# Statistics by channel tiles, the last q/k products behind v's third tile, the second mean's steps together: one change to a three-stage image kernel

## The chip, the cores and the metric

The kernel runs on one core of a Trainium2 chip. The metric is the device time of one execution in microseconds; a kernel's time is the median over several executions.

## What is computed

The input x has 384 channels of 192 x 192 pixels, in float32. Two layers follow each other, each with a residual sum, and each preceded by a group normalization without scale (32 groups of 12 channels).

```
def gn(v): ...                                   # 32 groups: (v - mean) / sqrt(var + 1e-5)

# layer 0, on gn(x)
qkv = einsum('bchw,oc->bohw', x, w_qkv) + b_qkv          # 1x1 convolution, 384 -> 1152
qkv = max over 2x2 pixels                                 # 96 x 96
qkv = depthwise 3x3 convolution(qkv) + b_dw
q, k, v = split(qkv)                                      # 8 heads of 48 channels, over 9216 pixels
attn = (q / |q|) @ (k / |k|)^T * temperature              # 48 x 48 per head
out = sum over i of a_i * topk_softmax(attn, k_i) @ v     # k_i = 24, 32, 36, 38
out = gelu(out), each pixel repeated 2x2
x = x + einsum(out, w_proj) + b_proj

# layer 1, on gn(x)
xb = sign(gn(x)), each channel moved by -3 to 3 pixels along the row
x = x + einsum(xb, sign(weight)) + bias
```

## The kernel before

**Units.** x is cut into 24 units of 8 rows (`UR`), 1536 pixels (`UPX`); a unit holds three channel tiles of 128 partitions (`CT`), 2304 KB in all. The order of the stages on the core is: statistics of x, one pass over all units for q and k, one pass for v (with the softmax in its first units and the attention products in the others), and a last stage that projects, takes signs, multiplies for layer 1 and stores.

**Statistics (L219 to L294).** Units are loaded from 23 down to 0, each as one transfer except the first and the last, which are loaded in three parts, one for each channel tile. Every third unit goes wholly to ScalarE (ACT), which runs Identity and Square over each tile with a running sum (L239); the others go wholly to VectorE (DVE) in nine `bn_stats` of 512 pixels (L248), and after every fourth such unit each tile is aggregated (L250). Sums of both kinds are put together in six DVE steps (L263 to L269), a product with the group indicator adds the channels of a group (`group_sums`, L198), a short chain makes mean and reciprocal deviation per group (L274 to L280, with `inv_sqrt`), and `spread` (L203) brings both back to channels. DVE scales the weights wq by the deviation (L287), the first tile first. The mean's share of the bias comes from nine tiny products of `wg` with `shift` (`bqps`, L293), and DVE adds it to bq (L294). The pools of this part are then closed, and their memory is used by the next one.

**The q/k pass (L353 to L436).** `qkv_unit` (L313) makes one channel tile m of one unit: three blocks of pixels, three accumulated products each (L321) into one of three PSUM buffers, a maximum over 2 x 2 pixels on DVE (L328) that evicts a block, the bias on ACT (L335), and the depthwise convolution of nine steps, the first on ACT (L342), eight on DVE (L344). The result is transposed in 32 x 32 blocks on DVE (L383), and 16 DMAs on the SP queue bring the blocks of q or k to where TensorE (PE) can read them (`moved`, L401). `products(u)` (L412) is the product of q and k over a unit's pixels, 12 matmuls accumulated in three PSUM banks `gram`; in the loop it is issued one unit late, and that of the last unit is left to `gathered()`.

**The v pass (L571 to L641).** The same `qkv_unit` with tiles m = 0 to 2 for v. In unit 0, after m = 1, `gathered()` (L440 on) issues the last products and copies `gram` to `gsb`, and `group_sums` of the projection's bias gives `bg1` (L630, L631). From unit 1 on `softmaxes` (L449 on) is advanced by one step after each tile; its first steps sum the squares `ssq` (L455) into memory that belonged to the q/k pass, take the reciprocal root, and make `rk` (L465 to L468).

**What sets the order.** Up to here the framework's scheduler orders the instructions of each engine by its own estimate of the time; what the program issues later may be put earlier. The end of the v pass (L642 to L660) and the last stage (L771 on) are marked `manual_schedule`: there each engine runs in the order of the program. `order` of the units in the last stage starts with the two of `FIRST`, whose projection is made at L648 to L657 in the qkv buffers.

**The second mean (L650 to L660).** After the last attention product PE does the projection of m = 0, then m = 1, then the group product of the attention's sums (`wg1` with `om`, L655), then m = 2, then `spread`; DVE makes `om` (L651), `gm` (L656), `nmean1` (L660), and adds each projected tile to x in two steps (L568). The signs (L723, on ACT) wait for `nmean1`.

**The last stage.** For each unit: `summed` projects three tiles (`yps`, L559) and adds them (L568); `signed` makes the signs on ACT, and GpSimd (POOL) moves some channels (L701 to L715); `finished` makes the layer-1 products (L743) and adds them (L751); `stored` (L757) stores a finished unit from the ACT queue, and refills its memory from the SP queue with a unit that is still to come. The first units are stored and refilled tile by tile. The last two units are stored tile by tile from the SP queue as each tile is done (L755).

Of the kernel before, what the change touches and what calls it, by code (L numbers as in the profile page):

```python
# [10 lines left out]
F32 = mybir.dt.float32  # L11
# [9 lines left out]
P = 128  # L21
C = 384
# [125 lines left out]
def conv_preact_kernel(ctx: ExitStack, tc: tile.TileContext, a: dict, out: bass.AP):  # L148
# [65 lines left out]
    osum = ap.tile([P, CT, NAB], F32, name="osum")  # L214
    aT = right("aT").tile([P, CT, C], F32, name="aT")
    wq = right("wq").tile([P, CT, 3 * C], F32, name="wq")


    kept = {}  # L219
    with tc.tile_pool(name="p1", bufs=1, side="right") as p1, tc.tile_pool(name="p1ps", bufs=2, space=PSUM) as psp:  # L220
        stats = [p1.tile([P, CT, BATCH * (UPX // 512) * 6], F32, name=f"stats{i}") for i in range(NB)]
        mv = p1.tile([P, CT, NB, 2], F32, name="mv")
        acc = p1.tile([P, CT, 2, NU // SHARE], F32, name="acc")
        wg = p1.tile([NG, 3 * C], F32, name="wg")
        seen = 0
        for i in range(NU):
            u = NU - 1 - i
            xt = unit(u, parts=CT if u in (0, NU - 1) else 1)
            if u < KEEP:
                kept[u] = xt  # L230
            if i == 0:
                nc.scalar.dma_start(small, a["small"])
                nc.scalar.dma_start(indT, a["indT"])
                nc.scalar.dma_start(wq, a["w_qkvT"].rearrange("(t p) o -> p t o", p=P))
            if i % SHARE == 0:
                for t in range(CT):
                    for k, f in enumerate((AF.Identity, AF.Square)):
                        junk = p1.tile([P, UPX], BF16, name="junk")
                        nc.scalar.activation(  # L239
                            junk, xt[:, t], f, accum_out=acc[:, t, k, i // SHARE : i // SHARE + 1]  # L240
                        )
            else:
                b, k = divmod(seen, BATCH)
                seen += 1
                for t in range(CT):
                    for j in range(UPX // 512):
                        at = (k * (UPX // 512) + j) * 6
                        nc.vector.bn_stats(stats[b][:, t, at : at + 6], xt[:, t, j * 512 : (j + 1) * 512])  # L248
                    if k == BATCH - 1:
                        nc.vector.bn_aggr(mv[:, t, b, :], stats[b][:, t, :])  # L250
# [11 lines left out]
        more = p1.tile([P, CT, 2], F32, name="more")  # L262
# [12 lines left out]
        gv = p1.tile([NG, 2], F32, name="gv")  # L275
        nc.vector.tensor_scalar_mul(gv[:, 0:1], gs[:, 0:1], -1.0)
        var = p1.tile([NG, 1], F32, name="var")
        nc.vector.scalar_tensor_tensor(var, gs[:, 0:1], gv[:, 0:1], gs[:, 1:2], ALU.mult, ALU.add)
        nc.vector.tensor_scalar_add(var, var, 1e-5)
        inv_sqrt(p1, gv[:, 1:2], var, 1, "s0", NG)  # L280
        ps = psp.tile([P, CT, 2], F32, name="spread")
        spread(ps, gv)
        nc.vector.tensor_copy(rstd0, ps[:, :, 1])

        for c0, c1 in ((0, P), (P, 2 * C), (2 * C, 3 * C)):
            for t in range(CT):
                nc.vector.tensor_scalar_mul(wq[:, t, c0:c1], wq[:, t, c0:c1], rstd0[:, t : t + 1])  # L287
        nc.vector.tensor_copy(nmean0, ps[:, :, 0])
        shift = p1.tile([NG, 1], F32, name="shift")
        nc.vector.tensor_mul(shift, gv[:, 0:1], gv[:, 1:2])  # L290
        ps = psp.tile([P, NM], F32, name="bqps")
        for m in range(NM):
            nc.tensor.matmul(ps[:, m : m + 1], wg[:, m * P : (m + 1) * P], shift, start=True, stop=True)  # L293
        nc.vector.tensor_add(bq, bq, ps)  # L294
# [17 lines left out]

    def qkv_unit(pqkv, xt, u, m, pl, parts):  # L313

# [3 lines left out]
        for r0, nr, c0, ncol in BLOCKS:  # L318
            ps = pqkv.tile([P, 512], F32, name="qkv")
            for t in range(CT):  # L320
# [32 lines left out]
    with tc.tile_pool(name="p2w", bufs=1, side="right") as wp, tc.tile_pool(  # L353
# [52 lines left out]
        def products(u):  # L406

            n, nk, q, k = of_unit(u)
            for i in range(nk):
                L = min(P, n * WP - i * P)  # L410
                for t in range(CT):
                    nc.tensor.matmul(  # L412
                        gram[t][:, : BN[t] * B],
# [157 lines left out]
    with ExitStack() as vs:  # L571
# [34 lines left out]
        for u in range(NU):  # L606
# [10 lines left out]
            for m in range(CT):  # L617
# [24 lines left out]
        with tc.manual_schedule():  # L642
# [13 lines left out]
            nc.vector.tensor_scalar(gm, ps, -1.0 / (GRP * NPX), bg1, ALU.mult, ALU.add)  # L656
# [3 lines left out]
            nc.vector.tensor_add(nmean1, nmean0, ps[:, :, 0])  # L660

    att.close()


    with end:
# [68 lines left out]
        def finished(i):  # L734
# [3 lines left out]
            for m in range(CT):  # L738
                for r0 in range(0, UR, 4):
# [118 lines left out]
```

## Time and profile before

| | before |
|---|---|
| median of 4 runs | 2288.18 us (2286.95 to 2289.35) |
| profiled execution | 2288.53 us |
| its span, first to last instruction | 2286.7 us |
| granted TensorE clock, mean | 0.966 |
| PE busy | 2099.9 us (92%), 6135 instructions |
| DVE busy | 1903.4 us (83%), 3269 |
| ACT busy | 819.3 us (36%), 1418 |
| POOL busy | 211.4 us (9%), 338 |
| DMA | 300.30 MB, 208727 packets, mean 131 GB/s |

The profile is of one execution. Times are in microseconds from the start of the span. In the timeline a row gives start, duration, engine, line and operation; "out<-in" are tiles of the program, "x13" says how many instructions of a kind were run together in the row, and in brackets stand the idle time of the engine before the row and what ended it. PE is TensorE's products, PEld its weight loads, and the ending q (SPq, ACTq) means a queue that issues DMAs. One matmul in float32 shows as two records on PE. "Granted clock" is the share of full speed that TensorE was given. The stages lie at 0 to 161 (statistics), 161 to 1346 (q and k), 1346 to 1968 (v) and from there to the end (last stage). One execution of an unchanged kernel differs from another by about 2 us, as the four runs show.

### The profile page before, as it was taken

Reading aid. Unit: us, or ns where it says so; the run is one execution under the profiler, and the core shown is the slowest. Engines: PE = TensorE matmul, PEld = TensorE weight load, DVE = VectorE, ACT = ScalarE, POOL = GpSimd, SP = SyncE. Lnnn points to the kernel's source line nnn. Section 1 sums busy time; section 2 is a strip of 40 time slices with the busy share of each in tenths; the row PEclk is TensorE's granted clock in tenths of the full one; section 3 lists DMA queues with packets and bytes.
Section 4 is the critical chain, followed back from the end, with each engine's and each line's share of the span. In section 5 each row is a group of like instructions: output and inputs, shape, how many; then the busy total and the mean of one; then the engine's idle time right before and its main releaser. Section 6 shows DMA issues by size and latency. Waiting matters only on the chain.

```text
span 2286.7 us, 19474 instructions
## 1 busy us (share of the span) xinstructions
PE 2099.9 (92%) x6135; PEld 993.2 (43%) x6135; DVE 1903.4 (83%) x3269; ACT 819.3 (36%) x1418; POOL 211.4 (9%) x338
## 2 busy tenths in 40 slices
PE   1029999999999999999999979999999999989998
PEld 0014444444444444444444434444444444445554
DVE  4667888888888888888888878986788887879998
ACT  5532222222222222222222212225323333487775
POOL 0000000000000000000000000000000000276674
PEclk7559999999999999999999989999999999999999
DMA  9962222222222232222222222004222212289996
GB/s 397 418 261 61 65 64 70 72 95 71 65 64 70 72 95 70 65 64 71 74 93 71 64 48 86 38 31 177 83 83 80 86 42 85 81 335 404 420 411 248
DMA packets 208727, 300.30 MB, mean 131 GB/s; under 512 B 162000, under 2 KB 164848, under 8 KB 208624
## 3 DMA queue, kind: packets, MB, share of 16 engines
q1 hardware_dynamic: 197936, 243.46, 30.6%
q10 hardware_dynamic: 10688, 55.61, 6.0%
q8 instruction: 48, 0.79, 0.1%
q14 instruction: 55, 0.45, 0.1%
HBM read 213.68 MB, written 56.62 MB: 118 GB/s over the span
## 4 chain that ended last, share of the span: by engine, by line
PE 77%; DVE 11%; DMA 8%; ACT 2%; issue 1%; SPq 1%; ACTq 0%; POOL 0%; POOLq 0%; DVEq 0%
PE qkv L321 65%; DMA xt<-in_x_dram 7%; PE l1ps L743 5%; DVE chunk L344 4%; PE yps L559 3%; PE gram L412 3%; DVE pooled L328 2%; PE ops L594 2%; DVE xt L568 2%; DVE dw L344 1%; DVE stats L248 1%; DMA out_dram<-xt 1%; ACT signs L723 1%; DVE xt L751 0%; SPq L401 0%
## 5 line engine op out<-in xcount | busy, mean ns | idle before, releaser
L321 PE MATMUL qkv<-xt,wq 128*128 128x512 f32 x3888 | 1681.9, 593 | 0.3 <-DVE small L294 0.3
L321 PEld LDWEIGHTS qkv<-xt,wq 128*128 128x128 f32 x3888 | 736.4, 190 | 920.2 <-issue 823.9
L344 DVE SCALAR_TENSOR_TENSOR dw<-pooled,small,dw 128x384 f32<-128x384 f32 (+2 forms) x1152 | 709.1, 616 | 118.8 <-ACT dw L342 93.7
L328 DVE TENSOR_REDUCE pooled<-qkv 128x128 f32<-128x512 f32 x648 | 442.9, 685 | 71.5 <-PE qkv L321 71.0
L344 DVE SCALAR_TENSOR_TENSOR chunk<-pooled,small,chunk 128x384 f32<-128x384 f32 (+3 forms) x696 | 370.5, 546 | 74.7 <-ACT chunk L342 57.3
L346 ACT COPY pooled<-pooled 128x196 f32<-128x196 f32 x207 | 73.6, 356 | 764.5 <-DVE dw L344 543.0
L335 ACT ACTIVATE pooled<-pooled,small 128x384 f32<-128x384 f32 x216 | 133.0, 616 | 407.6 <-DVE pooled L328 400.1
L723 ACT ACTIVATE signs<-xt,nmean 64x1536 fp8e4<-64x1536 f32 x144 | 226.5, 1573 | 63.2 <-PE yps L559 51.6
L743 PE MATMUL l1ps<-signs,wb 128*128 128x384 fp8e4 x864 | 150.5, 328 | 6.6 <-POOL signs L715 4.5
L568 DVE SCALAR_TENSOR_TENSOR xt<-yps,small,xt 128x768 f32<-128x768 f32 x132 | 127.9, 1013 | 25.6 <-PE yps L559 19.2
L559 PE MATMUL yps<-chunk,wpr 128*128 128x384 f32 x396 | 136.5, 490 | 6.9 <-DVE xt L568 6.9
L751 DVE SCALAR_TENSOR_TENSOR xt<-l1ps,small,xt 128x768 f32<-128x768 f32 x144 | 135.6, 1009 | 6.1 <-ACT signs L723 4.0
L248 DVE BATCH_NORM_STATS2 stats<-xt 128x6 f32<-128x512 f32 x144 | 87.2, 676 | 60.6 <-DMA xt<-in_x_dram 60.6
L198 PE MATMUL gsps<-sums,small 128*32 128x2 f32 x6 | 0.5, 196 | 128.2 <-DVE sums L269 128.2
L433 ACT ACTIVATE sq<-dw 128x384 bf16<-128x384 f32 (+2 forms) x144 | 75.3, 523 | 117.0 <-DVE dw L344 117.0
L743 PEld LDWEIGHTS <-wb 128*128 128x128 fp8e4 x864 | 84.1, 97 | 74.3 <-issue 16.4
L302 POOL MEMSET pooled<- 128x196 f32 x9 | 2.4, 265 | 1171.9 <-DVE dw L344 1154.4
L342 ACT ACTIVATE dw<-pooled,small 128x384 f32<-128x384 f32 (+2 forms) x144 | 100.5, 698 | 2.3
L559 PEld LDWEIGHTS yps<-chunk,wpr 128*128 128x128 f32 x396 | 72.6, 190 | 62.4 <-PE yps L559 15.6
L239 ACT ACTIVATE junk<-xt 128x1536 bf16<-128x1536 f32 x48 | 71.1, 1482 | 52.1 <-DMA xt<-in_x_dram 50.9
L383 DVE STREAM_TRANSPOSE blocks<-dw 128x384 f32<-128x384 f32 (+1 forms) x144 | 82.0, 569 | 3.4
L412 PE MATMUL gram<-room 128*128 128x160 f32 (+3 forms) x438 | 68.1, 309 | 15.4 <-DMA room<-blocks 15.4
(117 smaller groups left out, 640.4 us busy)
## 6 DMA issues: line engine op xcount, KB each, us to landing
xt<-in_x_dram SPq DMA_DIRECT2D x83, 2304.0 KB, 13.2
out_dram<-xt ACTq DMA_DIRECT2D x19, 2304.0 KB, 13.9
room<-blocks SPq DMA_DIRECT2D x736, 36.0 KB, 2.0
xt<-in_x_dram SPq DMA_DIRECT2D x18, 768.0 KB, 8.5
out_dram<-xt ACTq DMA_DIRECT2D x9, 768.0 KB, 7.9
out_dram<-xt SPq DMA_DIRECT2D x6, 768.0 KB, 6.6
wq<-in_w_qkvT_dram ACTq DMA_DIRECT2D x1, 1728.0 KB, 15.2
room<-blocks SPq DMA_DIRECT2D x32, 48.0 KB, 2.1
```

The lines of the kernel that those rows point to most:

```text
L248: nc.vector.bn_stats(stats[b][:, t, at : at + 6], xt[:, t, j * 512 : (j + 1) * 512])
L321: nc.tensor.matmul(ps, wq[:, t, m * P : (m + 1) * P], x4[:, t, r0 : r0 + nr, c0 : c0 + ncol], start=(t == 0), stop=(t == CT - 1),)
L328: nc.vector.tensor_reduce(pl[:, 2 + r0 // 2 : 2 + (r0 + nr) // 2, 1 + c0 // 2 : 1 + (c0 + ncol) // 2], ps.rearrange("p (i a j b) -> p i j ...
L335: nc.scalar.activation(new, new, AF.Identity, bias=bq[:, m : m + 1])
L342: nc.scalar.activation(acc2, src, AF.Identity, bias=bdw[:, m : m + 1], scale=wdw[:, m, 0:1])
L344: nc.vector.scalar_tensor_tensor(acc2, src, wdw[:, m, k : k + 1], acc2, ALU.mult, ALU.add)
L412: nc.tensor.matmul(gram[t][:, : BN[t] * B], q[:L, t, i], k[:L, B0[t] : B0[t] + BN[t], i], start=u == 0 and i == 0, stop=u == NU - 1 and i ...
L559: nc.tensor.matmul(ps, wpr[:, t, m * P : (m + 1) * P], o[:, t, :], start=(t == 0), stop=(t == CT - 1),)
L568: nc.vector.scalar_tensor_tensor(x5[:, m, r], yb, bpr[:, m : m + 1], x5[:, m, r], ALU.add, ALU.add)
L723: nc.scalar.activation(rows_of(sg, p, SAT[t] - HSHIFT[t][h]), xt[p, t, :].rearrange("p (r w) -> p r w", w=W), AF.Sign, bias=nmean1[p, t : ...
L743: nc.tensor.matmul(ps[:, j, : 2 * W], wb[:, t, m * P : (m + 1) * P], rows_of(sg, slice(0, P), SAT[t])[:, r0 + 2 * j : r0 + 2 * j + 2], sta ...
L751: nc.vector.scalar_tensor_tensor(blk, ps[:, :, : 2 * W], bl1[:, m : m + 1], blk, ALU.add, ALU.add)
```

## The change

Five things are edited:

- **Statistics by channel tiles.** In every unit, ACT takes tile t = u mod 3 and DVE the other two, instead of whole units to one of them. ACT's sums are scaled as they are made, and all sums go into one array `part`, which has a further column with 0 and the 1e-5; three DVE steps are left for the reduction. Unit 1, too, is loaded in three parts. `wg` is put into memory of the later `aT`, and `shift` into the pool `att`, so that both outlive this part.
- **The bias** becomes a function, called after the third block of the first tile of unit 0; its products go into a buffer of the qkv ring.
- **The last products** of q and k: `gathered()` is called after m = 2, not m = 1, and these products are kept in program order. In the order of instructions of the changed kernel, PE has all 27 matmuls of v's unit 0 and then the 12 products; before, it had one of the products ahead of m = 1 and eleven behind it. The products for `bg1` stand at the very start of the kernel.
- **The second mean**: after m = 0, `wg1` with `om` and `spread` follow each other; m = 1 and m = 2 come behind them, on PE and on DVE.
- **The last store**: the last tile of the last unit is stored in two halves of 384 KB, each after its own sum.

```
-            xt = unit(u, parts=CT if u in (0, NU - 1) else 1)
+            xt = unit(u, parts=CT if u in (0, 1, NU - 1) else 1)
...
-            if i % SHARE == 0:
-                for t in range(CT):
-                    for k, f in enumerate((AF.Identity, AF.Square)):
...
-                        nc.scalar.activation(
-                            junk, xt[:, t], f, accum_out=acc[:, t, k, i // SHARE : i // SHARE + 1]
-                        )
-            else:
-                b, k = divmod(seen, BATCH)
...
+            for t in range(CT):
+                if t == u % SHARE:
+                    at = NB + i // SHARE
+                    for k, f, scale in ((0, AF.Identity, measure), (1, AF.Square, measure**0.5)):
+                        junk = p1.tile([P, UPX], BF16, name="junk")
+                        nc.scalar.activation(junk, xt[:, t], f, scale=scale, accum_out=part[:, t, k, at : at + 1])
+                    continue
+                b, k = divmod(seen[t], BATCH)
+                seen[t] += 1
...
+                if k == BATCH - 1:
+                    nc.vector.bn_aggr(part[:, t, :, b], stats[b][:, t, :])
...
-        nc.vector.tensor_reduce(more, acc, AX.X, ALU.add)
-        nc.vector.tensor_mul(sq, mv[:, :, :, 0], mv[:, :, :, 0])
-        nc.vector.tensor_add(sq, sq, mv[:, :, :, 1])
-        nc.vector.tensor_reduce(sums[:, :, 0], mv[:, :, :, 0], AX.X, ALU.add)
-        nc.vector.tensor_reduce(sums[:, :, 1], sq, AX.X, ALU.add)
-        nc.vector.scalar_tensor_tensor(sums, more, 1.0 / (BATCH * UPX), sums, ALU.mult, ALU.add)
+        nc.vector.tensor_mul(sq, part[:, :, 0, :NB], part[:, :, 0, :NB])
+        nc.vector.tensor_add(part[:, :, 1, :NB], part[:, :, 1, :NB], sq)
+        nc.vector.tensor_reduce(sums, part, AX.X, ALU.add)
...
-        nc.vector.tensor_scalar_mul(gv[:, 0:1], gs[:, 0:1], -1.0)
+        nc.vector.tensor_scalar_mul(gv[:, 0:1], ps[:, 0:1], -BATCH / (NU * GRP))
...
-        nc.vector.tensor_scalar_add(var, var, 1e-5)
...
-        ps = psp.tile([P, NM], F32, name="bqps")
+    def bias(ps):
         for m in range(NM):
             nc.tensor.matmul(ps[:, m : m + 1], wg[:, m * P : (m + 1) * P], shift, start=True, stop=True)
         nc.vector.tensor_add(bq, bq, ps)
...
-    def qkv_unit(pqkv, xt, u, m, pl, parts):
+    def qkv_unit(pqkv, xt, u, m, pl, parts, before=None):
...
+        if before:
+            before(pqkv.tile([P, 512], F32, name="qkv")[:, :NM])
         new = pl[:, 2 : 2 + PR, 1 : 1 + WP]
         nc.scalar.activation(new, new, AF.Identity, bias=bq[:, m : m + 1])
...
+                    if u == NU - 1:
+                        tc.keep_in_program_order(ins)
...
-                qkv_unit(pqkv, xt, u, m, pool[m], [(acc, 0, n)])
+                qkv_unit(pqkv, xt, u, m, pool[m], [(acc, 0, n)], None if u or m else bias)
...
-                if u == 0 and m == 1:
+                if u == 0 and m == CT - 1:
                     gathered()
...
-            projected(pqkv.tile([P, 512], F32, name="qkv")[:, :PPX], FIRST[1], 1)
             ps = psp.tile([P, P], F32, name="p3ps")[:NG, :1]
             for t in range(CT):
                 nc.tensor.matmul(ps, wg1[:, t], om[:, t : t + 1], start=(t == 0), stop=(t == CT - 1))
             nc.vector.tensor_scalar(gm, ps, -1.0 / (GRP * NPX), bg1, ALU.mult, ALU.add)
-            projected(pqkv.tile([P, 512], F32, name="qkv")[:, :PPX], FIRST[1], 2)
             ps = psp.tile([P, P], F32, name="p3ps")[:, :CT].unsqueeze(2)
             spread(ps, gm)
             nc.vector.tensor_add(nmean1, nmean0, ps[:, :, 0])
+            for m in range(1, CT):
+                projected(pqkv.tile([P, 512], F32, name="qkv")[:, :PPX], FIRST[1], m)
...
-                if i + 2 >= NU:
+                    if i == NU - 1 and m == CT - 1:
+                        px = slice(r0 * W, (r0 + 4) * W)
+                        nc.sync.dma_start(ov[u, :, m, px], xt[:, m, px])
+                if i + 2 >= NU and (i, m) != (NU - 1, CT - 1):
                     nc.sync.dma_start(ov[u, :, m], xt[:, m])
```

More of the change, by code (lines that the diff above doesn't have):

```diff
@@ L215, in conv_preact_kernel @@
     aT = right("aT").tile([P, CT, C], F32, name="aT")
+    wg = aT.rearrange("p t c -> p (t c)")[:NG]
+    shift = ap.tile([NG, 1], F32, name="shift")
     wq = right("wq").tile([P, CT, 3 * C], F32, name="wq")
@@ L221, in conv_preact_kernel @@
         stats = [p1.tile([P, CT, BATCH * (UPX // 512) * 6], F32, name=f"stats{i}") for i in range(NB)]
[L222 to L225, printed above, removed]
+        part = p1.tile([P, CT, 2, NB + NU // SHARE + 1], F32, name="part")
+        measure = 1.0 / (BATCH * UPX)
+        nc.vector.memset(part[:, :, 0, NB + NU // SHARE :], 0.0)
+        nc.vector.memset(part[:, :, 1, NB + NU // SHARE :], 1e-5 * NU / BATCH)
+        seen = [0] * CT
         for i in range(NU):
             u = NU - 1 - i
-            xt = unit(u, parts=CT if u in (0, NU - 1) else 1)
+            xt = unit(u, parts=CT if u in (0, 1, NU - 1) else 1)
             if u < KEEP:
@@ L234, in conv_preact_kernel @@
                 nc.scalar.dma_start(wq, a["w_qkvT"].rearrange("(t p) o -> p t o", p=P))
-            if i % SHARE == 0:
-                for t in range(CT):
-                    for k, f in enumerate((AF.Identity, AF.Square)):
+            for t in range(CT):
+                if t == u % SHARE:
+                    at = NB + i // SHARE
+                    for k, f, scale in ((0, AF.Identity, measure), (1, AF.Square, measure**0.5)):
                         junk = p1.tile([P, UPX], BF16, name="junk")
-                        nc.scalar.activation(
-                            junk, xt[:, t], f, accum_out=acc[:, t, k, i // SHARE : i // SHARE + 1]
-                        )
-            else:
-                b, k = divmod(seen, BATCH)
[L244 to L250, printed above, removed]
+                        nc.scalar.activation(junk, xt[:, t], f, scale=scale, accum_out=part[:, t, k, at : at + 1])
+                    continue
+                b, k = divmod(seen[t], BATCH)
+                seen[t] += 1
+                for j in range(UPX // 512):
+                    at = (k * (UPX // 512) + j) * 6
+                    nc.vector.bn_stats(stats[b][:, t, at : at + 6], xt[:, t, j * 512 : (j + 1) * 512])
+                if k == BATCH - 1:
+                    nc.vector.bn_aggr(part[:, t, :, b], stats[b][:, t, :])
             if u == NU // 2:
@@ L261, in conv_preact_kernel @@
         sums = p1.tile([P, CT, 2], F32, name="sums")
-        more = p1.tile([P, CT, 2], F32, name="more")
-        nc.vector.tensor_reduce(more, acc, AX.X, ALU.add)
         sq = p1.tile([P, CT, NB], F32, name="sq0")
-        nc.vector.tensor_mul(sq, mv[:, :, :, 0], mv[:, :, :, 0])
-        nc.vector.tensor_add(sq, sq, mv[:, :, :, 1])
-        nc.vector.tensor_reduce(sums[:, :, 0], mv[:, :, :, 0], AX.X, ALU.add)
-        nc.vector.tensor_reduce(sums[:, :, 1], sq, AX.X, ALU.add)
-        nc.vector.scalar_tensor_tensor(sums, more, 1.0 / (BATCH * UPX), sums, ALU.mult, ALU.add)
+        nc.vector.tensor_mul(sq, part[:, :, 0, :NB], part[:, :, 0, :NB])
+        nc.vector.tensor_add(part[:, :, 1, :NB], part[:, :, 1, :NB], sq)
+        nc.vector.tensor_reduce(sums, part, AX.X, ALU.add)
         ps = psp.tile([NG, 2], F32, name="gsps")
@@ L288, in conv_preact_kernel @@
         nc.vector.tensor_copy(nmean0, ps[:, :, 0])
-        shift = p1.tile([NG, 1], F32, name="shift")
         nc.vector.tensor_mul(shift, gv[:, 0:1], gv[:, 1:2])
-        ps = psp.tile([P, NM], F32, name="bqps")
+    def bias(ps):
         for m in range(NM):
@@ L411, in products @@
                 for t in range(CT):
-                    nc.tensor.matmul(
+                    ins = nc.tensor.matmul(
                         gram[t][:, : BN[t] * B],
```

## The prediction

> **What bounds the kernel now.** I read the page first: its shares of time, its chain that ended last, then the timeline around each edited place, then the windows of granted clock and DMA share.
>
> ```profile
> PE 77%; DVE 11%; DMA 8%; ACT 2%; issue 1%; SPq 1%; ACTq 0%; POOL 0%; POOLq 0%; DVEq 0%
> ```
>
> This is the chain that ended last. TensorE sets the end for 77% of the span, and almost all of that is L321, the products of the two passes, which the change leaves as they are. The edits lie where another engine ends last: the statistics (DMA, then DVE), the passage from q/k to v (SP, DMA, DVE), the second mean (PE, DVE, ACT together) and the tail. So the change can win or lose a few microseconds at four joints. About 0.2%, 4.6 us of the median 2288.18, is what a measurement of this kernel can tell from no change.
>
> **Part 1, the start.** Timeline, columns start and duration:
>
> ```profile
> 140.31 7.81 DVE L248 BATCH_NORM_STATS2 stats<-xt 128x6 f32<-128x512 f32 x13 [5.85 <-DMA xt<-in_x_dram]
> ...
> 151.79 0.48 DVE L250 BATCH_NORM_AGGREGATE mv<-stats 128x2 f32<-128x72 f32 x1
> ...
> 155.59 1.44 PE L203 MATMUL spread<-gv,indT 32*128 32x2 f32 x6 [1.97 <-DVE gv L193]
> ...
> 156.89 3.97 PE L293 MATMUL bqps<-shift,wg 32*128 32x1 f32 x18
> ...
> 157.26 3.06 DVE L287 TENSOR_SCALAR wq<-wq,rstd 128x128 f32<-128x128 f32 x9
> ...
> 161.12 5.29 PE L321 MATMUL qkv<-xt,wq 128*128 128x512 f32 x8 [0.26 <-DVE small L294]
> ```
>
> DVE waits 5.85 us for unit 1, which comes in one piece, and then has 18 statistics of 0.604 us for units 1 and 0 in a row: the last aggregate ends at 152.27, although unit 0's parts had landed at 142.17, 144.06 and 145.93 (transfers of the trace). After the change unit 1 also comes in thirds, 1.88 us apart, and of each unit DVE has only two tiles. For unit 0 these are tiles 1 and 2: from 144.15, 3 x 0.604 = 1.81, an aggregate (0.38 from start to start), 1.81, and 0.48 for the last, so 148.63. That is 3.64 earlier. The third tile costs ACT 2 x 1.6 us per unit, beside a transfer of 5.65 us per unit, and unit 0's (landed 142.17) ends near 145.4: covered; if it were not, each 1.6 us would show. The five dependent reductions from 152.30 to 153.08 become three (about 0.6): 0.18. The scaled copy's use and the +1e-5 step (0.14 and 0.14, with gaps) leave the path: 0.25. The products of the spread thus end at 152.95, not 157.03.
>
> Then the bias: now 18 records (9 products) of 0.214 us stand between the spread and the first qkv, which waits for them through DVE's L294: 4.09 us. After, the first qkv needs only the first scaled tile of wq, which DVE ends 0.51 after the spread: start at 153.5 rather than 161.12, 7.6 earlier. The bias products come behind the nine qkv products of m = 0 and still take PE time: 2.0 us at full clock (half of 3.97; the warm L203 at 1984.24 gives 0.82 for 6 records, 2.5 for 18), 3.97 at half clock. They take a buffer of the qkv ring; DVE evicts m = 0 before the addition of bq, so nothing is queued long behind it. Leaves 5.6. Last, the clock: the granted clock is 0.50 in the window 161.00 to 164.34 and 1.00 behind it, and the changes in this trace (164.34, 1348.77, 1362.42, 2007.54, 2010.95) lie on a grid of 3.413 us. A start at 153.5 meets that grid so that full clock comes at 157.5: 4.0 us cold instead of 3.2, 0.4 lost. **Gain 5.2**, bounds 3.0 (bias cold, worst phase) and 6.0. Behind it TensorE is the chain without a break until 1282, so it all arrives.
>
> **Part 2, the passage to v.**
>
> ```profile
> 1345.95 10.25 SPq L401 DMA_DIRECT2D room<-blocks  x16
> ...
> 1359.08 0.30 DVE L455 TENSOR_REDUCE ss<-ssq 128x6 f32<-128x144 f32 x1 [11.22 <-DMA room<-blocks]
> ...
> 1359.09 0.87 PE L412 MATMUL gram<-room 128*128 128x160 f32 x2 [15.41 <-DMA room<-blocks]
> ...
> 1368.81 3.37 PE L412 MATMUL gram<-room 128*128 128x192 f32 x22
> ...
> 1379.94 0.69 DVE L328 TENSOR_REDUCE pooled<-qkv 128x128 f32<-128x512 f32 x1 [1.88 <-PE qkv L321]
> ...
> 1387.67 0.69 DVE L328 TENSOR_REDUCE pooled<-qkv 128x128 f32<-128x512 f32 x1 [0.22 <-PE qkv L321]
> ```
>
> SP issues 16 transfers in 10.25 us; until the last lands (1358.96) both PE, with a first gram product put ahead of v's m = 1, and DVE stand still. The order of instructions after the change has all 12 gram products behind m = 2. DVE's wait stays: its scratch takes the memory of the blocks that are still being sent. PE, though, can do m = 1 (7.73 us) at 1346.7, then has its three PSUM buffers full until DVE evicts the first, near 1364.6. From there: m = 2 7.73, gram 3.4, unit 1's m = 0 7.73, 0.2 to the first eviction of what is 1387.67 now: 1383.7 without a clock loss. But PE has then stood about 10 us, and rows say what that costs: 15.41 idle was followed by a granted clock of 0.50 in the window 1359.00 to 1362.40. One such window loses 1.7, two lose 3.4, so 1385.4 to 1387.1, 0.6 to 2.3 earlier. The bg step (0.14) leaves DVE ahead of the transposes. The other end: if only DVE counted, its five waits for PE (4.29) less what stays of them: 4.0. DVE carries the chain until about 1545, with short waits for ACT alone, and a gain there passes on. **Gain 1.6**, bounds 0.6 and 4.0; I stay near the PE path since it ends last.
>
> [...]
>
> **Part 3, the second mean.**
>
> ```profile
> 1982.11 2.20 PE L559 MATMUL qkv<-chunk,wpr 128*128 128x384 f32 x6
> ...
> 1983.54 0.20 DVE L656 TENSOR_SCALAR gm<-p3ps,bg 32x1 f32<-32x1 f32 x1
> 1984.24 0.82 PE L203 MATMUL p3ps<-gm,indT 32*128 32x1 f32 x6
> ...
> 1985.00 4.14 PE L559 MATMUL yps<-chunk,wpr 128*128 128x384 f32 x12
> 1986.21 0.15 DVE L660 TENSOR_TENSOR nmean<-nmean,p3ps 128x3 f32<-128x3 f32 x1
> 1986.44 15.96 ACT L723 ACTIVATE signs<-xt,nmean 64x1536 fp8e4<-64x1536 f32 x10 [5.31 <-issue]
> ...
> 2007.74 7.29 PE L743 MATMUL l1ps<-signs,wb 128*128 128x384 fp8e4 x34 [3.47 <-POOL signs L715]
> ```
>
> Put together, the mean's steps no longer wait for L568 of m = 1 and m = 2: wg at 1981.83 to 1982.18, gm 1982.4, spread to 1983.3, nmean 1983.3; the first sign starts at 1983.5, 2.9 earlier. The price is on PE: m = 1, which ran in the shadow of om, and m = 2 come after the spread (1983.3 to 1987.4), and the first yps takes m = 2's bank, so it waits for DVE's eviction of it (1.94): 1989.45 instead of 1985.00. Projections, the first layer-1 products (1997.58) and the first stores (issued at 2001.61, 2003.45, 2005.31) all come **4.45 later**. ACT's next signs stand behind these stores in its queue, but each unit gives ACT 2.7 us back (6 x 1.6 in 12.3). PE itself is level again by 2015: the wait of 3.47 for signs disappears. What isn't level is the DMA traffic:
>
> ```profile
> 2002.00:2010.00 8.00, 4.53 (x22) 2.23 (x21) 4.00 (x5) 7.88 (x6) 6.83 (x11) 0.85 0.93 305
> 2010.00:2020.00 10.00, 9.81 (x43) 5.57 (x42) 8.20 (x10) 9.83 (x7) 8.71 (x13) 0.95 0.95 348
> 2020.00:2030.00 10.00, 9.00 (x46) 5.17 (x46) 8.37 (x9) 9.84 (x7) 8.70 (x13) 1.00 0.95 367
> 2030.00:2045.00 15.00, 13.96 (x61) 7.74 (x59) 11.68 (x13) 12.09 (x8) 10.71 (x17) 1.00 0.99 382
> ```
>
> The last two columns are the DMA engines' share and GB/s. From the first store on they are full, and a unit's load issued at 2027.84 lands at 2044.60 with DVE waiting, as again at 2083.03, behind a store and a refill; from there to the end PE runs without a wait for data. Starting 4.45 late, the same bytes can make up only what the shares leave: 0.07 x 8 + 0.05 x 20 + 0.01 x 15 = 1.7. **Cost 2.8**, bounds -2.9 (only the earlier signs count) and +8.2 (below).
>
> **Part 4, the last store in halves.** The last six stores land 1.88 us apart up to 2285.69, the DMA share is 1.02 from 2275 to 2280, and the first half can go only about 1 us before 2279.84: the queue decides, **0**, bounds -0.9 (half of one transfer) and +0.4 (one more issue on SP, 0.35).
>
> [...]
>
> **The sum**: -5.2 - 1.6 + 2.8 + 0 = -4.0, against the profiled execution's 2288.53 (span 2286.7 and 1.8 around it) 2284.5. That execution is 0.35 above the median of the four runs; for a median I say **2284.3**.
>
> **Rivals.**
> 1. The delay behind the second mean is absorbed: PE is level at 2015, and the loads catch up before 2083. For it, the chain goes through ACT's signs, which come earlier; against it, shares of 0.93 to 1.01. -6.8: 2281.4.
> 2. The signs alone count; the stores' delay is nothing and the 2.9 arrive. -9.7: 2278.5. Against it: PE's own 4.45.
> 3. **Slower**: stores and refills that start late meet, and the queues stay at the mixed rate of 2002 to 2010 (305 at a share of 0.93, 328 at full share). The 12.9 MB of 2010 to 2045 (348 x 10 + 367 x 10 + 382 x 15) then take 39.3 us instead of 35. With the late start, 4.45 - 0.56 + 4.3 = 8.2: +1.4, 2289.6. It decides, slower than before, where the cost is above 6.8: a rate under 340 GB/s in that stretch, which averages 368 now.
> 4. The change doesn't shorten the start (DVE or ACT still ends as late, or the bias costs what it saved): +1.2, 2289.4.
>
> **Chances.** Forecast 55% (own range 2281.3 to 2287.3, two fifths of it under 2283.6, which is 0.2% faster); first rival 25%, second 6%, third 8% (a third of it above 2292.8), fourth 6%. Faster 0.22 + 0.25 + 0.06 = 0.53; slower 0.03; the rest, 0.44, within 0.2%. The range reaches from 2280.0, the first rival with its spread, to 2287.6, and leaves out the last three, 2 in 10.
>
> **What would show it.** Last aggregate at 148.6, first qkv near 153.5, bias products behind it; a rise of the granted clock near 157.5. Around 1340 PE works in SP's transfers, then stops about 10 us; the eviction of 1387.67 comes 0.6 to 2.3 earlier, counted from the last transpose. First sign 2.9 earlier and first layer-1 product 4.45 later against the last attention products; the two DVE waits for loads (2044.69, 2083.03) 2.8 later against the same. Wrong it would be above all where DMA's slack is larger than the shares say, or where the last products of v's first units go through DVE in an order other than I assume.

## The result, and the profile after

The changed kernel takes 2291.9 us (median of 29 executions), the kernel before 2288.4 (47): ratio 1.0018, 95% interval 1.0012 to 1.0023, so 2.7 to 5.3 us **slower**. The prediction had said 2284.3, with a range of 2280.0 to 2287.6. The profiled execution took 2291.64, its span is 2289.9, and the chain that ended last is again TensorE's for 77%.

The start, from the timeline of the changed kernel (start, duration, engine, line):

```profile
147.93 0.48 DVE L253 BATCH_NORM_AGGREGATE part<-stats 128x2 f32<-128x72 f32 x1
...
151.39 1.44 PE L203 MATMUL spread<-gv,indT 32*128 32x2 f32 x6 [1.69 <-DVE gv L193]
...
152.95 2.66 POOL L361 MEMSET blocks<- 128x3072 f32 x1 [151.64 <-PE spread L203]
153.06 5.50 DVE L284 TENSOR_SCALAR wq<-wq,rstd 128x128 f32<-128x128 f32 x9
...
155.94 9.55 PE L319 MATMUL qkv<-xt,wq 128*128 128x512 f32 x18 [3.11 <-DVE wq L284]
...
165.43 2.16 PE L291 MATMUL qkv<-shift,aT 32*128 32x1 f32 x18
```

The spread ends at 152.83, 4.2 earlier than before. But TensorE then waits 3.11 for DVE's scaling of wq, which takes 5.50 for its nine instructions instead of 3.06. GpSimd's clearing of `blocks` now lies beside it from 152.95 to 155.61, and DVE's first two scalings, taken one by one, end at 155.69 and 155.75. Before, the clearing lay behind the scaling (timeline of the kernel before):

```profile
160.98 2.66 POOL L361 MEMSET blocks<- 128x3072 f32 x1 [159.68 <-PE bqps L293]
```

m = 1 starts at 167.52 instead of 170.53, and the last transpose ends 2.9 earlier, at 1343.17.

The passage to v, changed kernel:

```profile
1343.80 9.56 PE L319 MATMUL qkv<-xt,wq 128*128 128x512 f32 x18 [3.31 <-DVE pooled L326]
...
1361.84 10.77 PE L319 MATMUL qkv<-xt,wq 128*128 128x512 f32 x18 [8.48 <-DVE pooled L326]
...
1372.45 3.64 PE L412 MATMUL gram<-room 128*128 128x160 f32 x24
```

TensorE makes m = 1 in the shadow of the transfers, stops 8.48 us, and makes m = 2 in 10.77 instead of some 7.8: the granted clock is 0.50 until 1367.5, for the first 5.6 us of it. From the last transpose to the first `rk` it is 41.3 us instead of 42.2, so 0.9 is won. DVE's `om` comes 3.8 earlier than before, at 1977.77 instead of 1981.58.

The second mean in the kernel before (its other rows are in the prediction):

```profile
1981.58 0.20 DVE L651 TENSOR_REDUCE om<-osum 128x3 f32<-128x54 f32 x1
...
1997.58 6.70 PE L743 MATMUL l1ps<-signs,wb 128*128 128x384 fp8e4 x38
```

And in the changed kernel:

```profile
1977.77 0.20 DVE L653 TENSOR_REDUCE om<-osum 128x3 f32<-128x54 f32 x1
...
1978.02 0.35 PE L656 MATMUL p3ps<-om,wg 128*32 128x1 f32 x6 [2.75 <-DVE om L653]
...
1978.67 1.44 PE L203 MATMUL p3ps<-gm,indT 32*128 32x1 f32 x6 [0.30 <-DVE gm L657]
1980.04 6.72 PE L561 MATMUL qkv<-chunk,wpr 128*128 128x384 f32 x12
...
1980.39 20.75 ACT L725 ACTIVATE signs<-xt,nmean 64x1536 fp8e4<-64x1536 f32 x13 [3.05 <-issue]
...
1988.89 4.11 PE L561 MATMUL yps<-chunk,wpr 128*128 128x384 f32 x12 [2.13 <-DVE xt L570]
...
2001.43 12.14 PE L745 MATMUL l1ps<-signs,wb 128*128 128x384 fp8e4 x72
```

Its windows there (the third number from the end is the granted clock):

```profile
1979.00:1981.00 2.00, 2.00 (x8) 1.68 (x8) 0.16 (x1) 0.61 (x1) 0.00 (x0) 0.50 0.00 0
1981.00:1985.00 4.00, 4.00 (x8) 2.18 (x7) 0.72 (x1) 3.95 (x3) 2.32 (x4) 0.50 0.01 2
```

TensorE has nothing to do while it waits 2.75 for `om`. The tiny products behind that stop, and then m = 1 and m = 2, run mostly at half clock (granted 0.50 from 1978.45 to 1985.28): 6.72 us for 12 records that take 4.14 at full clock. Then the first `yps` waits 2.13 for m = 2's buffer. The first layer-1 product starts at 2001.43, which is 23.66 behind `om`; before, it was 16.00.

From there the chain that ended last goes through the store and the refill of one tile of the first unit, with TensorE waiting 6.02 for what hangs on it (chain of the changed kernel, start and length):

```profile
2009.16 7.77 DMA out_dram<-xt
...
2017.02 8.72 DMA xt<-in_x_dram
...
2025.85 0.09 DVE xt L570
```

The windows of the changed kernel from its first store on (last three columns: granted clock, DMA share, GB/s):

```profile
2006.00:2014.00 8.00, 8.00 (x49) 4.80 (x47) 8.00 (x10) 4.40 (x3) 2.64 (x4) 1.00 0.94 306
2014.00:2024.00 10.00, 8.57 (x35) 4.61 (x34) 4.56 (x5) 9.82 (x8) 8.68 (x13) 1.00 1.03 429
2024.00:2034.00 10.00, 5.22 (x19) 2.65 (x19) 6.75 (x7) 9.36 (x6) 8.71 (x13) 0.66 0.91 312
2034.00:2049.00 15.00, 14.80 (x63) 8.31 (x62) 13.14 (x14) 10.16 (x7) 9.27 (x14) 1.00 1.01 404
2049.00:2057.00 8.00, 7.80 (x38) 4.21 (x37) 7.58 (x9) 7.88 (x6) 6.14 (x9) 1.00 0.94 362
```

GB/s times length, summed, is 18.8 MB in these 51 us. Before, the 51 us from 2002 on (the windows shown in the prediction and one more, 422 GB/s from 2045 to 2053) moved 18.7 MB: the same bytes in the same time, 4 us later. The rates are spread otherwise (429 and then 312), but the start that came late isn't made up in these windows. The clock is part of the picture: behind the wait of 6.02 it is 0.50 from 2026.24 to 2033.07, which shows as 0.66 in the third row. Before, it was 0.50 only from 2007.54 to 2010.95 between the first layer-1 product and the last.

### The profile page after: what moved, and what is told of

The parts are those of the page before. It is cut to its first block, busy times and chain, and to the rows that moved or that the text cites. A ratio compares the mean times of both kernels' runs of the same rounds, so it can differ in the third digit from the quotient of the medians.

```text
span 2289.9 us, 19485 instructions
## 1 busy us (share of the span) xinstructions
PE 2106.0 (92%) x6135; PEld 994.5 (43%) x6135; DVE 1907.1 (83%) x3267; ACT 819.7 (36%) x1418; POOL 213.9 (9%) x338
## 4 chain that ended last, share of the span: by engine, by line
PE 77%; DVE 12%; DMA 7%; ACT 1%; issue 1%; SPq 0%; ACTq 0%; POOLq 0%; DVEq 0%; POOL 0%
PE qkv L319 63%; DMA xt<-in_x_dram 6%; PE l1ps L745 5%; DVE chunk L344 5%; PE yps L561 3%; PE gram L412 3%; DVE pooled L326 2%; DVE xt L570 2%; PE ops L596 2%; DVE dw L344 1%; DMA out_dram<-xt 1%; DMA wq<-in_w_qkvT_dram 1%; ACT chunk L342 0%; ACT pooled L335 0%; DVE xt L753 0%
## 5 line engine op out<-in xcount | busy, mean ns | idle before, releaser
L703 POOL COPY rest<-signs 9x384 int32<-9x384 int32 (+1 forms) x144 | 72.7, 505 | 92.3 <-ACT signs L725 86.5
```

## The experiments

Each was measured beside the kernel before. no_mean_again is no_mean's kernel a second time, and no_mean_filled, in spite of its name, is mean_filled's kernel a second time. L is the time from `om` to the first layer-1 product, W what TensorE then waits up to 2255 (stops over 0.3 us, added up from the trace), both of the profiled execution. Differences between kernels are of ratios, times 2288; with these intervals most of them are known to about 3 us.

| kernel | median | ratio to before (95%) | L | W |
|---|---|---|---|---|
| before | 2288.4 | 1 | 16.00 | 8.3 |
| changed | 2291.9 | 1.0018 (1.0012 to 1.0023) | 23.66 | 7.4 |
| only_mean | 2293.2 | 1.0024 (1.0014 to 1.0034) | 20.23 | 6.5 |
| no_mean | 2284.4 | 0.9986 (0.9977 to 0.9994) | 17.41 | 6.9 |
| mean_filled | 2290.9 | 1.0010 (1.0001 to 1.0019) | 20.53 | 9.0 |
| memset_late | 2287.6 | 1.0003 (0.9994 to 1.0012) | 23.86 | 6.9 |
| only_start | 2285.5 | 0.9991 (0.9981 to 1.0000) | 17.41 | 5.0 |
| only_pin | 2286.4 | 0.9993 (0.9984 to 1.0001) | 16.00 | 7.0 |
| late_stores | 2293.7 | 1.0022 (1.0013 to 1.0031) | 21.87 | 7.9 |
| no_halves | 2285.1 | 0.9985 (0.9975 to 0.9994) | 17.41 | 7.2 |
| start_mended | 2280.3 | 0.9968 (0.9956 to 0.9980) | 17.41 | 5.5 |
| start_pin_m1 | 2280.1 | 0.9962 (0.9949 to 0.9974) | 19.11 | 7.8 |
| best_ring | 2278.4 | 0.9956 (0.9944 to 0.9969) | 15.99 | 8.2 |
| no_mean_filled | 2290.7 | 1.0008 (0.9999 to 1.0016) | 20.53 | 8.9 |
| no_mean_again | 2285.2 | 0.9986 (0.9977 to 0.9995) | 17.41 | 6.7 |
| late_10 | 2288.5 | 1.0001 (0.9992 to 1.0010) | 19.64 | 5.8 |
| late_40 | 2292.4 | 1.0020 (1.0011 to 1.0029) | 26.34 | 6.9 |
| only_mean_filled | 2293.9 | 1.0025 (1.0015 to 1.0035) | 18.60 | 9.4 |

**only_mean and no_mean: the second mean alone, and everything but it.** The edit of only_mean is the change's own hunk at L650 to L660 on the kernel before; no_mean is the changed kernel without that hunk.

> The kernel before with the second mean's steps put together and nothing else. Theory: the loss of the change is made here. The changed kernel's trace shows the first layer-1 product 7.65 us later than before, counted from om (DVE L651), and DVE's wait for a load at 2083 7.1 later. If it needs nothing of the other edits: 2288.4 + 7.1 = 2295.5, with m = 1 and m = 2 at half clock (12 records in 6.7 us instead of 4.1). Rival: it needs the clock windows to lie as the other edits place them; then full clock, 4.45 later at the first layer-1 product and 2291.2.

> The changed kernel with the second mean's steps in the order of before. Theory: the start keeps its 2.9 and the passage to v its 0.9, both read from the changed kernel's trace, and nothing is lost behind: 2288.4 - 3.8 = 2284.6. Rival: the start and the passage are absorbed behind 1968 by transfers that are not ready earlier; then 2287 to 2288.4.

only_mean is 1.0024, some 5.5 us slower; no_mean 0.9986, 3.2 faster, and so again in its second measurement. The loss is thus made by this edit, and the theories hold for the place. Its size is 0.32%, 7.3 us, between no_mean and the changed kernel. In only_mean TensorE is at half clock too (granted 0.52 from 1984.0 to 1987.5), but the first `yps` doesn't wait for m = 2's buffer: the bias's tile, which turns the ring of three qkv buffers by one, is missing there. So L is 4.2 longer and not 7.7. In no_mean that tile alone makes L 1.4 longer than before.

**mean_filled: the stop filled.**

```
             nc.vector.tensor_reduce(om, osum, AX.X, ALU.add)
+            ps = psp.tile([P, P], F32, name="p3ps")
+            for t in range(CT):
+                for k in range(4):
+                    nc.tensor.matmul(ps, wpr[:, t, :P], wpr[:, t, k % CT * P : (k % CT + 1) * P], start=True, stop=True)
```

> The changed kernel with 12 extra products (128 x 128 of a weight with itself, into a PSUM tile that is then overwritten, their results used by nothing) in TensorE's 2.75 us stop between m = 0 and the group product. Theory: the stop is what takes the clock to half; filled, the spread and m = 1 and m = 2 run at full clock, 3.2 us less (6.72 to 4.14 and 1.44 to 0.82), and of these nearly all reach the end: 2288.8 to 2289.3. Rival: the delay is made by the order alone and the late stores hide the clock: 2291.9 as the changed kernel.

Timeline of this kernel, and two of its windows:

```profile
1975.46 2.84 PE L657 MATMUL p3ps<-wpr 128*128 128x128 f32 x24
...
1979.84 4.14 PE L561 MATMUL qkv<-chunk,wpr 128*128 128x384 f32 x12
...
1986.11 4.11 PE L561 MATMUL yps<-chunk,wpr 128*128 128x384 f32 x12 [2.13 <-DVE xt L570]
...
1977.00:1980.00 3.00, 2.54 (x25) 2.28 (x24) 1.58 (x5) 0.68 (x2) 0.00 (x0) 1.00 0.38 160
1980.00:1984.00 4.00, 3.98 (x12) 2.04 (x12) 2.02 (x3) 3.76 (x3) 1.52 (x4) 1.00 0.03 6
```

With the stop filled, the clock stays at 1.00 and m = 1 and m = 2 take 4.14: the stop is what cost the clock. L falls by 3.13 to 20.53, 4.53 more than before, which is the prediction's 4.45 for the order and the buffer. But the time fell less: to 1.0010, and to 1.0008 when the same kernel was measured again:

> Again the changed kernel with TensorE's stop in the second mean filled by extra products, beside kernels of this call, since its first measurement (2290.9, interval 1.0001 to 1.0019) doesn't tell the two cases apart. Theory as revised by the late stores' run: the first layer-1 product comes 3 earlier, and all of it arrives: 2288.9. Rival: the transfers hold the end: 2291.9.

Both together are about 2 us under the changed kernel, neither the theory's value nor the rival's. In mean_filled's profile W is 1.6 longer, most of it a wait of 2.81 for a load near 2085. Behind that wait the clock is at 0.50 once more, from 2087.97 to 2091.39, and the stretch up to the last product is 1.3 longer beyond L and W. So in this execution what the clock gave in the second mean was lost again later on. On the kernel before the filling gave nothing that can be told from noise:

> The kernel before with the second mean's steps put together and TensorE's stop filled by 12 extra products, so at full clock and with the qkv ring's buffers as before. Measured without the filling: 1.0024, 5.3 more than before, first layer-1 product 4.2 late counted from om. Filled, m = 1 and m = 2 take 4.2 instead of 5.8, so the product is 2.6 late. Theory 1: before + 2.6, 2290.8. Rival: the order costs 5 whatever the clock, as the filled changed kernel suggests (1.0009 against 1.0018): 2293.

It took 1.0025 against 1.0024 without, each to 0.0010: the rival's value, not theory 1's. L fell by 1.6, and W rose by 2.9. So the clock explains 3.1 of L in the changed kernel, and between nothing and 2 us of the time.

**late_stores, late_10, late_40: only the first layer-1 product is late.** On no_mean, with `range(10)`, `range(20)` or `range(40)`:

```
+                if i == 0:
+                    ps = psp.tile([P, 2, 512], F32, name="l1ps")
+                    for k in range(20):
+                        nc.tensor.matmul(ps[:, 0, :P], wpr[:, k % CT, :P], wpr[:, k % CT, P : 2 * P], start=True, stop=True)
                 finished(i)
```

> The changed kernel with the second mean as before (2284.4) and 20 extra products (128 x 128, their results used by nothing) between the projections and the first layer-1 product, some 4.7 us of TensorE and nothing else: signs are not earlier, only the first unit's layer-1 products, its stores and refills are later. Theory: the transfers from 2002 to 2083 are one full queue and make up nothing of a late start: 2284.4 + 4.7 = 2289.1, or at least 2288.4. Rival (the prediction's step): 1.7 of it is made up, 2287.4; second rival: all is made up since TensorE waited 3.47 for signs of the second unit, 2284.4.

> As late_stores, with 10 extra products ahead of the first layer-1 product instead of 20, some 2.4 us. Theory 1 (a late first product passes on one to one): baseline + 2.4, 2286.8. Theory 2 (it falls behind a step of the transfers, a unit's load ordered behind other traffic, and costs a fixed amount beyond its lateness): baseline + 5 to 7, about 2290. Theory 3 (the prediction: up to 1.7 is made up): baseline + 0.7, 2285.1.

> As late_stores, with 40 extra products, some 9.4 us. Theory 1: baseline + 9.4, 2293.8, and the kernel with 20 (measured 2293.7) was then out of line. Theory 2: baseline + 12 to 14, 2297 to 2298. Theory 3: baseline + 7.7, 2292.1.

> The changed kernel with the second mean as before, again, as the baseline of this call for the two late kernels: 2284.4 as before, 0.9986.

L is 2.2, 4.5 and 8.9 longer than no_mean's. The time is longer by 0.15%, 0.36% and 0.34%, 3.4, 8.2 and 7.8 us, each to about 3 us: 19.4 in all for 15.6 of lateness. Theory 1, one to one, fits late_10 and late_40, and the middle one lies over it, by about the error; theory 2's fixed extra doesn't fit late_40. With 1.7 made up in each, as the prediction had it, the three would add up to 10.5, and that doesn't show. The table says the same: W lies between 5.0 and 9.4 in all profiles, while L goes from 16 to 26, and W doesn't fall as L rises. What is left, last product less `om` less L less W, is 272.3 to 274.5 in each. Where W lies in its band isn't settled, but the traces show what goes with it. In late_10 and late_stores, as in the changed kernel and only_mean, a wait of 5.1 to 6.5 us for the first unit's refill is followed by 6.8 us at half clock; in both measurements of no_mean that wait is 4.7 or less, and the clock is down for 3.4 us. In late_40, which showed no surplus, it is 3.4 too. In late_stores' profile the last store also lands 1.5 later behind the last product than elsewhere. This fits a late start that costs a little more than itself, and no run tests it alone.

**memset_late: the clearing held back.**

```
+            if gate:
+                edge = wq[:, CT - 1, 3 * C - 2 * (PR + 3) :].rearrange("p (r w) -> p r w", w=2)
+                nc.gpsimd.tensor_copy(t[:, :, :: WP + 1], edge)
...
+        nc.gpsimd.tensor_copy(blocks[:, 0, :1], wq[:, CT - 1, 3 * C - 1 :])
         nc.gpsimd.memset(blocks, 0.0)
-        pool = padded(wp, 2 * CT)
+        pool = padded(wp, 2 * CT, gate=True)
```

> The changed kernel with GpSimd's clearing of blocks and pooled held back until DVE has scaled the last part of wq (seven tiny copies of wq go ahead of it on GpSimd). Theory: GpSimd's 2.66 us clearing of blocks, which in the changed kernel lies beside the scaling, is what makes the first scaling of a 128 x 128 part take 2.63 us instead of 0.28; held back, the first qkv product starts near 153.6 instead of 155.94 and all that follows is 2.0 to 2.4 earlier: 2289.5 to 2289.9. Rival: the scaling is slow because wq's last part or the spread's results come late; then it stays at 2.6 and the time at 2291.9 or, with the clearing late for the first transposes, above.

Timeline of this kernel:

```profile
153.13 3.05 DVE L284 TENSOR_SCALAR wq<-wq,rstd 128x128 f32<-128x128 f32 x9
153.68 4.67 PE L322 MATMUL qkv<-xt,wq 128*128 128x512 f32 x7 [0.78 <-DVE wq L284]
...
157.35 2.65 POOL L365 MEMSET blocks<- 128x3072 f32 x1
```

The scaling is back at 3.05, the first 128 x 128 part at 0.29 instead of 2.62, and the first qkv starts at 153.68: the prediction had said 153.5. The theory holds. m = 1 starts at 165.09, 5.4 earlier than before. The time fell by 0.15%, 3.4 us, with an error of some 2 to 3. That is more than the theory's 2.4; in this profile the clock also came back sooner in the passage (m = 2 in 9.55 instead of 10.77).

**only_start and only_pin: the two edits that gain, each alone.** only_start is no_mean without the move of `gathered()`, the pin and the halved store; only_pin is the kernel before with that move and pin.

> The kernel before with the first two edits alone (statistics by channel tiles, the bias behind m = 0). Theory: last aggregate 3.6 to 3.9 earlier, but the first scaling of wq stands for 2.6 us behind GpSimd's clearing of blocks, so m = 1 starts 2.4 to 3.0 earlier (170.53 before) and all of that arrives: 2288.0 - 2.7 = 2285.3. Rival: the start also moves the places where the granted clock falls later on, and gives back or gains up to 1.7 at each; then the passage (last transpose to first rk, 42.2 before) or the second mean (om to first layer-1 product, 16.0 before) differ by more than 0.7.

> The kernel before with the last products alone moved behind m = 2 and kept in program order. Theory: TensorE does m = 1 in the shadow of SP's transfers, stops some 8 us, and then makes m = 2 at half clock for one to two windows; last transpose to first rk goes from 42.2 to between 39 and 41.6, as in the changed kernel's trace (41.3) and in the one with the clearing held back (39.0): 2288.0 - 0.6 to - 3.2, the value by the middle 2286.3. Rival: DVE sets the pace here and order on TensorE gives nothing: 42.2 and 2288.0.

only_start gains 2.1 (m = 1 starts 2.1 earlier), only_pin 1.6 (last transpose to `rk` 39.65 instead of 42.2); both intervals reach to about no change, so each alone isn't shown by its time. The rival of the first is there in part: without the pin the passage took 43.0, 0.8 more, and L is 1.4 longer by the ring that the bias turns.

**no_halves: the store in one piece again,** on no_mean.

> The changed kernel with the second mean as before (2284.4) and the last tile stored in one piece as before. Theory: the last stores stand in a full queue and land 1.88 us apart, halves or not: 2284.4, and the time from the last layer-1 product to the end of the last store unchanged. Rival: the smaller last piece ends sooner by up to half a transfer, then this kernel is 0.9 later, 2285.3.

0.9985 against 0.9986, and from the last layer-1 product to the last landing 6.92 against 7.02: halves give nothing by the trace, and nothing that the times could tell.

**start_mended, start_pin_m1, best_ring: a better kernel.** start_mended is no_mean with the gates of memset_late. start_pin_m1 has `gathered()` behind m = 1 as before, but pinned. best_ring makes the bias in three tiles of the ring:

```
-                if u == 0 and m == CT - 1:
+                if u == 0 and m == 1:
...
+        for c0 in range(0, NM, CT):
+            ps = tile()
+            for m in range(c0, c0 + CT):
+                nc.tensor.matmul(ps[:, m - c0 : m - c0 + 1], wg[:, m * P : (m + 1) * P], shift, start=True, stop=True)
+            nc.vector.tensor_add(bq[:, c0 : c0 + CT], bq[:, c0 : c0 + CT], ps)
```

> The changed kernel with the second mean as before and GpSimd's clearing held back behind the scaling of wq. Theory: the two repairs add up, since all that is earlier at the first layer-1 product arrives at the end: 2284.4 - 4.3 (2291.9 to 2287.6 by the clearing alone) = 2280.1; by the trace's 2.4 of the start alone, 2282.0. Rival: the transfers behind 2002 set the end and take the gain: 2284.4.

> As start_mended, and the last products pinned behind m = 1 instead of m = 2. Theory: TensorE makes m = 1 in the shadow of SP's transfers, the 12 products as soon as these have landed, while it would wait for DVE's evictions, and m = 2 follows at full clock; last transpose to first rk about 38 (DVE's work alone) instead of 41.3: 1 to 3 earlier than start_mended, 2278 to 2281. Rival: DVE's order then is another (copies of gram ahead of evictions) and holds TensorE's buffers; not under 41, and no gain.

> As start_pin_m1, with the bias in three tiles of the qkv ring instead of one (three products and one sum each), so that the ring's three buffers stand as before at the second mean. Theory: the first yps tile then no longer needs the buffer of m = 2; om to first yps goes from 4.87 back to 3.42, the first layer-1 product is 1.4 earlier unless signs hold it, and 0.5 to 1.4 arrive: 2277 to 2280. Rival: signs of the first unit come last there, and nothing is gained.

The passage of best_ring:

```profile
1354.35 3.71 PE L418 MATMUL gram<-room 128*128 128x160 f32 x24 [2.43 <-DMA room<-blocks]
...
1359.25 8.24 PE L324 MATMUL qkv<-xt,wq 128*128 128x512 f32 x18 [1.19 <-DVE pooled L331]
```

The last products run while TensorE would wait for evictions, stops are 2.43 and 1.19, and m = 2 starts at full clock. Last transpose to `rk` is 36.6 instead of 41.3. best_ring is at 0.9956: 2278.4 us, 10 less than before and 14 less than the changed kernel. Of the three steps the first is clear (0.9968 against 0.9986); the other two are each within the error of the step, though the traces show what they were to do (36.4 and 36.6 in the passage, L back at 15.99).

## Why the prediction was wrong

**Part 1** gave 5.2; 2.1 to 2.9 came. The aggregates (148.41 against 148.6), the spread (152.83 against 152.95) and the bias products (2.16 against 2.0) were right. The step that failed is "after, the first qkv needs only the first scaled tile of wq, which DVE ends 0.51 after the spread": that tile took 2.62 us beside GpSimd's clearing, and 0.29 without. With the clearing out of the way m = 1 started 5.4 earlier in memset_late and 4.1 in start_mended, about the 5.2 that I had added up. I had listed what the first qkv no longer waits for, but not what GpSimd was waiting for: the clearing was held by the end of the bias products, and came free with them. A row of the kernel before could have told me the price, had I read it (timeline, near 1359):

```profile
1359.24 1.06 POOL L530 MEMSET full<- 128x1152 f32 x1
...
1359.42 0.91 DVE L456 TENSOR_SCALAR ss<-ss 128x6 f32<-128x6 f32 x1
```

Six elements per partition took 0.91 us, to the end of GpSimd's memset. In memset_late, where DVE comes first, the same step takes 0.17:

```profile
1353.92 0.17 DVE L462 TENSOR_SCALAR ss<-ss 128x6 f32<-128x6 f32 x1
...
1354.05 1.06 POOL L536 MEMSET full<- 128x1152 f32 x1 [0.17 <-issue]
```

In both kernels GpSimd's memset takes 1.06. Where it starts first, the DVE step lasts until it ends, to 1360.33 against 1360.30; where the DVE step starts first, it takes 0.17. What made DVE stand, no view shows.

The 0.4 that I took off for the clock rested on the places where it changed in one execution. They lie elsewhere in another: the rise came at 164.34 before, 159.15 in the changed kernel and 156.56 in memset_late, which are not whole multiples of 3.413 apart.

**Part 2** gave 1.6 with bounds of 0.6 and 4.0; 0.9 in the changed kernel's profile, 1.6 in only_pin's time and 2.5 in its profile. The mechanism was right: m = 1 in the shadow, then a stop and a cold m = 2.

**Part 3** gave a cost of 2.8; it is 7.3, between no_mean and the changed kernel, and this turned the sign. Three steps:
- The delay of 4.45 from order and buffer was right: 4.53 at full clock. Of it 1.4 is the bias's tile in the ring, which no_mean pays as well.
- The half clock was left out: it adds 3.1 to L. I weighed the clock for the start and the passage, and put it at nothing here, though moving m = 1 behind the mean opens a stop here as well: 2.75 us of it, with 1.8 us of tiny products behind, were followed by a granted clock of 0.50 for 6.8 us.
- "Starting 4.45 late, the same bytes can make up only what the shares leave" is the step that failed: nothing was made up when the first layer-1 product alone was late (19.4 us lost for 15.6 of lateness). In the changed kernel's trace the chain doesn't go through all bytes but through the store and refill of one tile (7.77 and 8.72), which begin with the first layer-1 sums. That room in the share of DMA was no slack on that path is my reading of this chain; the three late kernels show only that the lateness arrives. So the first rival (all absorbed) falls, and so does the second: the signs came 2.2 earlier than before, counted from `om`, and the kernel was slower. The fourth falls too, since the start did get shorter. The third, slower rival had the right side and, by coincidence, nearly the right price (8.2), but not the cause: it had the transfers stay slow, at 328 GB/s, and the 35 us from 2014 on moved 385, more than the 368 of before.

Beside no_mean L grew by 6.25, and the time by 7.3. The rest of about 1 is within the error.

**Part 4**, nothing, was right by the trace: from the last layer-1 product to the last landing it took 6.92 with the store in one piece and 7.02 in halves, which shows nothing of the 0.9 that the lower bound allowed.

With these terms (ratios of only_start and only_pin, and the mean's 7.3) the sum is -2.1 - 1.6 + 7.3 = 3.6; measured 4.1. The 7.3 is itself a difference from the changed kernel, so this tests only that the first two gains add up (3.7, and no_mean gained 3.2).

## What to carry to other kernels

When an edit lets work start earlier, ask of every engine what that work had been holding back; here GpSimd's clearing came free and fell beside the scaling. Taking a product out of a stop on TensorE can delay what follows twice, by its own time and by the clock behind the stop; here these were 3.1 each of L beside no_mean, though filling the stop gave back 2 us of the time at most. Where a stage begins with a store whose refill is waited for, look at its start as a link of a chain: here a late start reached the end in full, although the share of DMA seemed to leave room, while an earlier one was partly lost in later waits.

## What the runs showed of the hardware

- A DVE scaling in float32 beside a GpSimd memset stood until that ended: 2.62 us instead of 0.29 (128 x 128), 0.91 instead of 0.17 (128 x 6). DVE's maximum out of PSUM didn't: 0.69 us beside the clearing of memset_late, as elsewhere.
- A TensorE stop of 2.75 us, followed by 1.8 us of products with 32-wide operands, was followed by a granted clock of 0.50 for 6.8 us (1978.45 to 1985.28); the same stretch filled with 24 records of 128 x 128 kept it at 1.00.
- A TensorE stop of 8.48 us in the passage ended at 1361.84, and the granted clock stayed at 0.50 until 1367.5: 5.6 us of work at half clock behind one stop.
